# Attention with a residual on one core: the loads of x go to a step's last quarter, and one exchange round goes ahead of a result's stores

## The chip, the core and the metric

The kernel runs on one core of a Trainium2 chip. The core has a matrix engine (TensorE, "PE" in the profile; "PEld" are its weight loads), a vector engine (VectorE, DVE), a scalar engine (ScalarE, ACT), GpSimd (POOL) and SyncE (SP). SyncE computes nothing here; nearly every DMA is issued from its queue ("SPq"). All engines run side by side and wait for each other through semaphores. The metric is the device time of one execution in microseconds (us).

## The reference, cut to what matters

x has the shape (8, 512, 512): 8 batches of 512 positions by 512 features, float32. There are 16 heads of 32 features.

```python
Q = split_heads(x @ Wq.T + bq)
K = split_heads(x @ Wk.T + bk)
V = split_heads(x @ Wv.T + bv)
tQ = split_heads(tokens @ Wq.T + bq)      # one token per batch, from cond
tK = split_heads(tokens @ Wk.T + bk)
scores = einsum('bhqd,bhkd->bhqk', Q + tQ, K + tK) / sqrt(32)
attn = softmax(scores, axis=-1)
out = einsum('bhqk,bhkd->bhqd', attn, V)
return x + merge_heads(out)
```

## The kernel before

**Steps and quarters.** The work is cut into 32 steps, t = 0 to 31. Step t belongs to batch b = t // 4 and to a group of four heads, r = t % 4 (128 features, one head on each 32 partitions). A loop (L1000) runs steps 1 to 28; the first and the last steps are written out by hand. A step has four quarters, i = 0 to 3. Each quarter has one "item" on TensorE (part of the projections q, k or v of the next batch, or "V", the weighted sum of the values of step t - 1), and around it work for two other steps:

- `row_max` (L550) computes the scores of step t + 1 for 128 query rows, four heads side by side (matmuls L579), and VectorE reduces them to row maxima `nmax` (L546, L588). `denominators` (L620) then has ScalarE take the exponentials with that maximum and sum them (L634).
- `exponentials` (L681) computes the scores of step t a second time, transposed, with the row maxima subtracted by a small matmul (L686, which reads `maxT`), and ScalarE writes the exponentials `e` (L700). They are the moving operand of "V" in the next step (`times_v`, matmuls L709).
- `maxT` comes from GpSimd, which splits the maxima into bfloat16 parts (`split_max`, L642 to L651), and a transposing DMA on SyncE's queue (`turn_max`, L660).

**The blocked steps.** For t = 3, 7, ..., 27 (`BLOCKED`, L71; called u below, r = 3) the second computation of the scores is saved. The exponentials of `denominators` are kept in a big tile `blocks`. VectorE transposes it in 32 x 32 blocks (`turn_blocks`, L594, instruction L599, eight per step), and DMAs then exchange blocks between the partition groups (`swap_blocks`, L604, DMAs L618). The exchange is done in two halves. Each half has three rounds of six DMAs of 128 KB: round 0 copies blocks aside into `between`, round 1 copies the opposite blocks over them, round 2 copies `between` to the free places. A round's DMAs need those of the round before. Only when all six rounds have landed can "V" of step u begin, which is the last item of step u + 1 (there the items are q, k, v, V; in all other steps V, q, k, v). The table `SWAPS` (L991) says at the end of which quarter a round is recorded: the key is (t - u, i), the value (half, round).

```python
    SWAPS = {
        (-1, 2): (0, 0),
        (-1, 3): (0, 1),
        (0, 0): (0, 2),
        (0, 3): (1, 0),
        (1, 0): (1, 1),
        (1, 1): (1, 2),
    }
```

**x.** A block of x (128 features of a batch, 512 positions) is loaded by four DMAs of 64 KB into one of three buffers (`load_block`, L164, DMAs L170). VectorE transposes it into `xT` (`turn_x`, L345, instruction L351), and the call that has turned block n then loads block n + 3 into the buffer that has come free. In the loop, `turn_x` is called twice at the end of quarter 0 of the steps with r = 0 (that is step u + 1) and r = 1. GpSimd forms sums of parts of `xT` for the projections (`combine_x`, L354).

**Results.** After "V", VectorE transposes the result (`send`, L770, instruction L773), GpSimd multiplies by the reciprocal of the sums and adds the residual `xr` (L774, L775), and four DMAs store it (L778). The residual of step t + 1 (x with the bias of v) is loaded by four DMAs (`load_residual`, L179, DMAs L188) at the end of step t, and GpSimd adds the bias (L196).

**Who sets the order.** The order on TensorE, ScalarE, VectorE and GpSimd is the order in which the program is written (`manual_schedule`). SyncE's queue is not in that list: the framework places its DMAs, near where they are recorded. The queue is in order, and each DMA also waits for the one that stands eight places ahead of it to land.

Of the kernel before, what the change touches and what calls it, by code (L numbers as in the profile page):

```python
# [17 lines left out]
def kernel(  # L18
# [38 lines left out]
    nc = tc.nc  # L57
# [8 lines left out]
    NC = D // P  # L66
# [50 lines left out]
    def banks(i, n=1):  # L117

        row = row_of[0] or [at_end[j] for j in TURNS[turn[0]]]
        j = row[i]  # L120
        if n == 1:
            return psum[:, j, :]
        k = row[i + 1]
        return psum[:, j : k + 1 : k - j, :]
# [4 lines left out]
    def advance():  # L129
        turn[0] += 1  # L130
# [29 lines left out]
    def spread(a, d):  # L160

        return a.rearrange("(f j) d -> j f d", j=BL)[:, :, d : d + BL]

    def load_block(n):  # L164

        b, cc = divmod(n, NC)
        if b < B:
            xs[n] = xp.tile([P, NB, BL], F32, tag="x", name=f"x_{n}")
            for h in range(HG):
                nc.sync.dma_start(xs[n][h * BL : (h + 1) * BL], spread(x[b], cc * P + h * BL))  # L170
# [4 lines left out]
    def turned_by_vector(t):  # L175

        return t < T - 1

    def load_residual(t):  # L179

        b, g = divmod(t, G)
        if turned_by_vector(t):
            if late:
                xr[t] = late[0][:, 2, :].rearrange("p (f e) -> p f e", e=BL)
            else:
                xr[t] = op.tile([P, NB, BL], F32, tag="xr", name=f"xr_{t}")
            for h in range(HG):
                nc.sync.dma_start(  # L188
                    xr[t][h * BL : (h + 1) * BL], spread(x[b], g * P + h * BL)
                )  # L190
            bias = bvs[:, g, :].unsqueeze(1).broadcast_to([P, NB, BL])
        else:

            xr[t] = xT[b][:, g, :]
            bias = bvl.broadcast_to([P, S])
        nc.gpsimd.tensor_tensor(xr[t], xr[t], bias, ALU.add)  # L196
# [75 lines left out]
    for i in range(NS):  # L272
        r = slice(i * BL, (i + 1) * BL)
# [71 lines left out]
    def turn_x(n):  # L345
        b, cc = divmod(n, NC)
        if b >= B:
            return
        if cc == 0:
            xT[b] = xtp.tile([P, NC, S], F32, tag="xT", name=f"xT_{b}")  # L350
        nc.vector.transpose(xT[b][:, cc, :], xs[n].rearrange("p f i -> p (f i)"))  # L351
        load_block(n + 3)

    def combine_x(b, half, on=nc.vector):  # L354

        if b >= B:
            return
        blk = [[xT[b][:, i * 2 : i * 2 + 2, j * HS : (j + 1) * HS] for j in range(2)] for i in range(2)]
        to = [xc[:, i, :, :] for i in range(4)]
        if half == 0:  # L360
            on.tensor_tensor(to[2], blk[1][1], blk[0][1], ALU.subtract)
            on.tensor_tensor(to[1], to[2], blk[0][0], ALU.add)
        else:
            on.tensor_tensor(to[0], blk[0][1], blk[0][0], ALU.subtract)
            on.tensor_tensor(to[3], blk[1][0], to[1], ALU.subtract)
# [238 lines left out]
    def swap_blocks(t, half, move):  # L604

        def part(a, g):
            e = blocked[t][a * BL : (a + 1) * BL, g, half * 2 : half * 2 + 2]
            return e.rearrange("p c h s -> p (c h s)")

        if move == 0:  # L610
            between[t, half] = [
                ep.tile([P, 2, S], F32, tag="e", name=f"between_{t}_{half}_{i}") for i in range(2)
            ]
        for n, (a, g) in enumerate(APART):
            at = (n + 2) % HG * BL
            kept = between[t, half][n // HG][at : at + BL].rearrange("p i s -> p (i s)")
            to, of = [(kept, part(a, g)), (part(a, g), part(g, a)), (part(g, a), kept)][move]
            nc.sync.dma_start(to, of)  # L618
# [83 lines left out]
    def times_v(t, kc, pt, chunks=range(NS)):  # L702
        b, g = divmod(t, G)
        for j in range(HG):
            if t in BLOCKED:
                e = blocked[t][:, :, :, j, kc * BL : (kc + 1) * BL].rearrange("p a c e -> p c a e")
            else:
                e = es[t, kc, j // 2][:, j % 2, :]
            nc.tensor.matmul(  # L709
                pt[j * HD : (j + 1) * HD, :],  # L710
                vs[b % 2][:, kc, (g * HG + j) * HD : (g * HG + j + 1) * HD],
                e,
                start=(kc == chunks[0]),
                stop=(kc == chunks[-1]),
            )
# [13 lines left out]
    def masked(t):  # L729

        if t in aparts:
            return aparts.pop(t)
        apart = op.tile([P, HG, NS, NS], F32, tag="apart", name=f"apart_{t}")
        nc.gpsimd.tensor_tensor(
            apart,
            sums[t].rearrange("p c h o -> p h c o").broadcast_to([P, HG, NS, NS]),
            which.unsqueeze(1).unsqueeze(1).broadcast_to([P, HG, NS, NS]),
            ALU.mult,
        )
        return apart  # L740
# [16 lines left out]
    def weighted(t, pt, pd, between):  # L757

        apart = masked(t)
        for kc in range(NS):
            times_v(t, kc, pt)
            if kc == 0:
                spread_sums(apart, pd)
        rec = reciprocals(t, pd)
        between()
        send(t, pt, rec)
# [123 lines left out]
    split_max(0)  # L892
    first_products("k", 0, 1, lambda: denominators(0, 3), nothing, 2, 3)
    turn_x(NC)
    advance()
    row_max(1, 0)
    transpose_max(0, banks(1), nc.scalar.copy)
    other_products("k", 0, 1, lambda: denominators(1, 0), nothing, (0, 2))
    turn_x(NC + 1)
    load_residual(0)  # L900
    advance()

# [37 lines left out]
    row_max(1, 1)  # L940
    first_products("v", 0, 0, lambda: denominators(1, 1), nothing, 1)
    turn_x(NC + 2)
    load_residual(1)
    turn_x(NC + 3)
    advance()
    exponentials(0, 1)
    row_max(1, 2)
# [35 lines left out]
    def turn_more(t, i, late):  # L983

        for u in (t, t + 1):
            if u in BLOCKED:
                n = turned.get(u, 0)
                turned[u] = n + TURNED[t + 1 - u][i][late]
                turn_blocks(u, range(n, turned[u]))

    SWAPS = {  # L991
        (-1, 2): (0, 0),
        (-1, 3): (0, 1),
        (0, 0): (0, 2),
        (0, 3): (1, 0),
        (1, 0): (1, 1),
        (1, 1): (1, 2),
    }

    for t in range(1, T - 3):  # L1000
        b, r = divmod(t, G)
        blocks = t in BLOCKED
        w = 0 if blocks else HG
        items = ["q", "k", "v", "V"] if t - 1 in BLOCKED else ["V", "q", "k", "v"]
        for i, item in enumerate(items):
            rows = (t + 1, i + 1) if i < 3 else (t + 2, 0)
            begin(w)
            if not blocks:
                exponentials(t, i)
            late_first = item in ("v" if blocks else "qkv") and t % 2 == 1  # L1010
            hold = row_max(*rows, late_first, w)

            def held(i=i, hold=hold):
                hold()
                if i == 2:
                    split_max(t + 1)
                    turn_max(t + 1)

            dens = lambda: denominators(*rows, w)
            if item in "qkv":  # L1020
                products(t, item, blocks, held, dens, nothing)
            else:
                held()
                dens()
                if blocks:
                    weighted(t - 1, banks(4), banks(5), lambda: turn_more(t, i, 0))
                    released(6, 7, 0, 1, 2, 3, 5, 4)
                else:
                    weighted(t - 1, banks(0), banks(1), lambda: turn_more(t, i, 0))
                    released(2, 3, 1, 4, 5, 6, 7, 0)  # L1030
            if i == 0:
                if r == 0:
                    turn_x(t + NC + 2)
                    turn_x(t + NC + 3)
                if r == 1:
                    turn_x(t + NC + 3)
                    turn_x(t + NC + 4)
                if r == 1:
                    combine_x(b + 1, 1, nc.gpsimd)
            if i == 1 and r == 0:  # L1040
                combine_x(b + 1, 0, nc.gpsimd)
            if i == 2:
                aparts[t] = masked(t)
            if i == 3:
                load_residual(t + 1)
            turn_more(t, i, 1)
            for u in (t - 1, t, t + 1):
                if u in BLOCKED and (t - u, i) in SWAPS:
                    swap_blocks(u, *SWAPS[t - u, i])
    row_of[0] = None  # L1050

    def latest_pair(of, among):
# [64 lines left out]
    t = T - 3  # L1117
# [19 lines left out]
    t = T - 2  # L1137
# [26 lines left out]
    t = T - 1  # L1164
# [47 lines left out]
    b, g = divmod(t, G)  # L1212
# [55 lines left out]
```

## Time and profile before

| | us |
|---|---|
| median of 3 runs | 719.58 (717.72 to 719.66) |
| the profiled execution, its own time | 720.05 |
| its span in the trace | 718.0 |
| PE busy | 685.8 (96%) |
| VectorE busy | 563.6 (79%) |
| ScalarE busy | 563.2 (78%) |
| GpSimd busy | 233.2 (32%) |
| DMA queue of SyncE and ScalarE, share of the 16 DMA engines' time | 45.5% |

The profile is of one execution, whose time is 0.47 us above the median of the runs; 2.05 us of it lie outside the span. A busy time says how long an engine had an instruction in it, not that it was at its peak. "Idle before, releaser" is the time in which an engine stood still ahead of an instruction, and what the trace shows to have ended it; with a wait for several semaphores it is the one that came last by the profile. PEclk is the clock that TensorE was granted, 1.00 being full speed.

### The profile page before, as it was taken

What the parts mean: (1) busy time and instruction counts of PE and PEld (TensorE: products, weight loads), DVE (VectorE), ACT (ScalarE), POOL (GpSimd) and SP (SyncE); (2) the same over time, 40 slices, a digit from 0 to 9 for tenths busy, and PEclk for the clock granted to TensorE, in tenths of its full rate; (3) what the DMA queues carried; (4) which work ended last, traced back from release to release, by engine and by line L of the source; (5) the groups of instructions that cost most, each with busy time, mean ns of one, the idle gap of its engine ahead of it and who ended that gap; (6) DMA issues with size and microseconds to landing.
All of it is one profiled execution on the core that took longest, in us unless ns stands there. A gap on an engine that the chain in (4) does not pass through costs nothing.

```text
span 718.0 us, 22033 instructions
## 1 busy us (share of the span) xinstructions
PE 685.8 (96%) x8824; PEld 314.0 (44%) x8824; DVE 563.6 (79%) x878; ACT 563.2 (78%) x1427; POOL 233.2 (32%) x315
## 2 busy tenths in 40 slices
PE   9999999979999899989999899998999999999997
PEld 7444444424445344443444444443444445444432
DVE  3798798846988579884798857986689976987677
ACT  2589888858878688895888967888687998888664
POOL 3711323314243142421424233142431424231271
PEclk9999999999999999998999999999999999999999
DMA  6632426625267333673337723467225543177311
GB/s 178 106 54 47 68 36 151 140 61 82 42 146 150 67 65 75 127 156 55 58 70 133 163 48 57 99 125 148 47 46 116 121 101 63 34 152 148 53 31 30
DMA packets 231674, 65.50 MB, mean 91 GB/s; under 512 B 221834, under 2 KB 222346, under 8 KB 231572
## 3 DMA queue, kind: packets, MB, share of 16 engines
q1 hardware_dynamic: 229812, 63.05, 45.5%
q8 instruction: 69, 1.13, 0.7%
q10 hardware_dynamic: 1760, 1.05, 0.5%
q14 instruction: 33, 0.27, 0.1%
HBM read 19.75 MB, written 8.39 MB: 39 GB/s over the span
## 4 chain that ended last, share of the span: by engine, by line
PE 76%; SPq 7%; DMA 6%; POOL 4%; DVE 2%; ACT 2%; issue 2%; DVEq 0%; POOLq 0%; ACTq 0%
PE psum L435 30%; PE psum L709 16%; PE psum L579 13%; PE psum L689 9%; PE psum L686 4%; DMA maxT<-split 3%; SPq L618 2%; PE psum L378 2%; SPq L778 2%; SPq L170 2%; ACT psum L634 1%; DMA blocks<-between 1%; DVE nmax L546 1%; DMA xr<-in_x_dram 1%; POOL res L775 1%
## 5 line engine op out<-in xcount | busy, mean ns | idle before, releaser
L634 ACT ACTIVATE psum<-psum,nmax 128x512 f32<-128x512 f32 x368 | 244.5, 673 | 29.0 <-DVE nmax L546 21.5
L700 ACT ACTIVATE e<-psum 128x512 f32<-128x512 f32 x376 | 194.1, 603 | 91.2 <-PE psum L689 87.7
L546 DVE TENSOR_REDUCE nmax<-psum 128x1 f32<-128x512 f32 x298 | 191.3, 683 | 83.8 <-PE psum L579 81.4
L579 PE MATMUL psum<-kT,qT 32*128 32x512 f32 x1024 | 143.0, 605 | 0.0
L588 DVE TENSOR_REDUCE nmax<-psum 128x2 f32<-128x1024 f32 x101 | 122.5, 1213 | 1.3 <-PE psum L579 1.3
L689 PE MATMUL psum<-qT,kT 32*128 32x512 f32 x752 | 96.7, 587 | 0.0
L709 PE MATMUL psum<-e,v 128*32 128x512 f32 x800 | 95.3, 597 | 0.0
L196 POOL TENSOR_TENSOR xr<-xr,bvs 128x512 f32<-128x512 f32 x30 | 38.4, 1280 | 165.7 <-DMA xr<-in_x_dram 165.7
L774 POOL TENSOR_TENSOR res<-res,recs 128x512 f32<-128x512 f32 x30 | 31.4, 1047 | 179.3 <-DVE res L773 168.8
L579 PEld LDWEIGHTS psum<-kT,qT 32*128 32x128 f32 x1024 | 60.4, 182 | 53.1 <-issue 24.2
L634 ACT ACTIVATION_READ_ACCUMULATOR psum<-psum,nmax 128x1 f32 x368 | 78.8, 214 | 0.0
L634 ACT ACTIVATE blocks<-psum,nmax 128x512 f32<-128x512 f32 x112 | 76.1, 717 | 0.0
L599 DVE STREAM_TRANSPOSE blocks<-blocks 128x1024 f32<-128x1024 f32 x56 | 68.5, 1223 | 0.0
L709 PE MATMUL psum<-blocks,v 128*32 128x512 f32 x224 | 33.6, 741 | 17.9 <-ACT psum L634 10.9
L435 PE MATMUL psum<-wc_v,xc 128*32 128x256 f32 x768 | 50.2, 379 | 0.0
L435 PE MATMUL psum<-xc,wc_q 128*32 128x256 f32 x720 | 47.1, 379 | 0.0
L435 PE MATMUL psum<-xc,wc_k 128*32 128x256 f32 x720 | 47.1, 379 | 0.0
L686 PE MATMUL psum<-maxT,onesb 3*128 3x512 bf16 x376 | 37.1, 385 | 7.1 <-DMA maxT<-split 7.1
L709 PEld LDWEIGHTS psum<-e,v 128*32 128x32 f32 x800 | 20.8, 110 | 51.4 <-issue 29.2
L773 DVE STREAM_TRANSPOSE res<-psum 128x512 f32<-128x512 f32 x28 | 20.1, 717 | 29.1 <-PE psum L709 26.1
L775 POOL TENSOR_TENSOR res<-res,xr 128x512 f32<-128x512 f32 x30 | 38.5, 1283 | 2.4
L689 PEld LDWEIGHTS psum<-qT,kT 32*128 32x128 f32 x752 | 37.4, 185 | 1.7
(179 smaller groups left out, 877.4 us busy)
## 6 DMA issues: line engine op xcount, KB each, us to landing
between<-blocks SPq DMA_DIRECT2D x84, 128.0 KB, 2.4
blocks<-blocks SPq DMA_DIRECT2D x84, 128.0 KB, 2.3
blocks<-between SPq DMA_DIRECT2D x84, 128.0 KB, 2.4
out_dram<-res SPq DMA_DIRECT2D x122, 64.0 KB, 1.9
xr<-in_x_dram SPq DMA_DIRECT2D x120, 64.0 KB, 2.4
x<-in_x_dram SPq DMA_DIRECT2D x112, 64.0 KB, 2.4
w_q<-in_L_cond_Wq_dram SPq DMA_DIRECT2D x4, 256.0 KB, 4.8
w_v<-in_L_cond_Wv_dram SPq DMA_DIRECT2D x16, 64.0 KB, 2.3
```

The source lines that it names most:

```text
L196: nc.gpsimd.tensor_tensor(xr[t], xr[t], bias, ALU.add)
L435: nc.tensor.matmul(pt[r], still[:, r], moving, start=(kc == kcs[0]), stop=(kc == kcs[-1]))
L546: nc.vector.tensor_reduce(nmax[t][:, qc, j : j + 1, 0], pt, AX.X, ALU.max, negate=True)
L579: nc.tensor.matmul(pt, qkT["q", t][r, qc * P : (qc + 1) * P], qkT["k", t][r, :], start=True, stop=True,)
L588: nc.vector.tensor_reduce(nmax[t][:, qc, pr * 2 : pr * 2 + 2, 0], pt, AX.X, ALU.max, negate=True)
L599: nc.vector.transpose(e, e)
L634: nc.scalar.activation(to, of, AF.Exp, bias=nmax[t][:, qc, j, :], accum_out=sums[t][:, qc, j, :],)
L686: nc.tensor.matmul(bank[j], onesb[r, :], maxT[t][r, :], start=True, stop=False)
L689: nc.tensor.matmul(bank[j], qkT["k", t][r, kc * P : (kc + 1) * P], qkT["q", t][r, :], start=False, stop=True,)
L700: nc.scalar.activation(e[:, i, :], bank[pr * 2 + i], AF.Exp)
L709: nc.tensor.matmul(pt[j * HD : (j + 1) * HD, :], vs[b % 2][:, kc, (g * HG + j) * HD : (g * HG + j + 1) * HD], e, start=(kc == chunks[0]), ...
L775: nc.gpsimd.tensor_tensor(y, y, xr.pop(t), ALU.add)
```

## The change

`turn_x` no longer loads; it puts the number of the next block into a list, and `load_blocks` issues the loads of that list. In the loop `load_blocks` is called at the end of quarter 3 of every step. The two `turn_x` of the steps with r = 1 go from the end of quarter 0 to the end of quarter 2. Round 2 of the exchange's first half is recorded at the end of step u - 1, directly behind round 1, where it was recorded at the end of quarter 0 of step u. In a blocked step, the call of `turn_more` inside "V" is replaced by an empty one; by the table `TURNED` it turned no block there. Ahead of the loop each `turn_x` is directly followed by a `load_blocks`.

```diff
         nc.vector.transpose(xT[b][:, cc, :], xs[n].rearrange("p f i -> p (f i)"))
-        load_block(n + 3)
+        to_load.append(n + 3)
+
+    to_load = []
+
+    def load_blocks():
+        while to_load:
+            load_block(to_load.pop(0))
...
     SWAPS = {
-        (-1, 2): (0, 0),
-        (-1, 3): (0, 1),
-        (0, 0): (0, 2),
-        (0, 3): (1, 0),
-        (1, 0): (1, 1),
-        (1, 1): (1, 2),
+        (-1, 2): [(0, 0)],
+        (-1, 3): [(0, 1), (0, 2)],
+        (0, 3): [(1, 0)],
+        (1, 0): [(1, 1)],
+        (1, 1): [(1, 2)],
     }
...
                 if blocks:
-                    weighted(t - 1, banks(4), banks(5), lambda: turn_more(t, i, 0))
+                    weighted(t - 1, banks(4), banks(5), nothing)
...
-            if i == 0:
-                if r == 0:
-                    turn_x(t + NC + 2)
-                    turn_x(t + NC + 3)
-                if r == 1:
-                    turn_x(t + NC + 3)
-                    turn_x(t + NC + 4)
-                if r == 1:
-                    combine_x(b + 1, 1, nc.gpsimd)
+            if i == 0 and r == 0:
+                turn_x(t + NC + 2)
+                turn_x(t + NC + 3)
+            if i == 0 and r == 1:
+                combine_x(b + 1, 1, nc.gpsimd)
             if i == 1 and r == 0:
                 combine_x(b + 1, 0, nc.gpsimd)
+            if i == 2 and r == 1:
+                turn_x(t + NC + 3)
+                turn_x(t + NC + 4)
+            if i == 3:
+                load_blocks()
...
-                    swap_blocks(u, *SWAPS[t - u, i])
+                    for swap in SWAPS[t - u, i]:
+                        swap_blocks(u, *swap)
```

More of the change, by code (lines that the diff above doesn't have):

```diff
@@ L899 @@
     turn_x(NC + 1)
+    load_blocks()
     load_residual(0)
@@ L942 @@
     turn_x(NC + 2)
+    load_blocks()
     load_residual(1)
     turn_x(NC + 3)
+    load_blocks()
     advance()
@@ L1030 @@
                     released(2, 3, 1, 4, 5, 6, 7, 0)
-            if i == 0:
-                if r == 0:
-                    turn_x(t + NC + 2)
-                    turn_x(t + NC + 3)
-                if r == 1:
-                    turn_x(t + NC + 3)
-                    turn_x(t + NC + 4)
-                if r == 1:
-                    combine_x(b + 1, 1, nc.gpsimd)
+            if i == 0 and r == 0:
[3 more added lines that the diff above has]
+                combine_x(b + 1, 1, nc.gpsimd)
             if i == 1 and r == 0:
                 combine_x(b + 1, 0, nc.gpsimd)
+            if i == 2 and r == 1:
+                turn_x(t + NC + 3)
+                turn_x(t + NC + 4)
+            if i == 3:
+                load_blocks()
             if i == 2:
```

## The prediction

> **What bounds the kernel now.** First I asked what TensorE, busy 96% of the span, waits for. The waits of TensorE are three large groups and little else (us in total, times, longest):
>
> ```profile
> PE psum L709 <- ACT psum L634: 10.9, 3, 4.0
> PE psum L686 <- DMA maxT<-split: 7.1, 7, 1.8
> PE psum L709 <- DMA blocks<-between: 7.0, 2, 3.5
> ```
>
> The page's chain gives TensorE 76%, but a chain also runs through work that a short wait hangs on, so it does not size anything. I cut the loop instead into batches, each from the start of "V" of a blocked step to the next such start (TensorE's columns: stretch, its length, busy us and instructions, granted clock, DMA share, GB/s):
>
> ```profile
> 149.17:236.67 87.50, 83.17 (x1105) 0.98 0.49 96
> 236.67:324.55 87.88, 83.26 (x1105) 0.97 0.49 96
> 324.55:413.72 89.17, 84.28 (x1105) 0.97 0.49 95
> 413.72:500.55 86.83, 81.56 (x1105) 1.00 0.50 97
> 500.55:583.66 83.11, 83.11 (x1105) 0.98 0.45 91
> 583.66:666.30 82.64, 81.49 (x1109) 1.00 0.47 89
> ```
>
> The same instructions take 81.5 us of TensorE where the clock is full. The last two batches have almost no gap; the first four end with one. VectorE is busy 66 to 69 us and ScalarE 67 to 72 us of a batch, so a batch of 81.5 us is TensorE's own. The timeline shows where the gaps lie: ahead of "V" of u = 3, 7, 11, 15 and 19, never of u = 23 and 27. For u = 3 and u = 23, SyncE's queue and then TensorE (start, us, what; in brackets the idle before):
>
> ```profile
> 128.76 3.71 SPq L618 DMA_DIRECT2D between<-blocks  x6
> 132.57 1.17 SPq L618 DMA_DIRECT2D blocks<-blocks  x2
> 134.29 5.02 SPq L170 DMA_DIRECT2D x<-in_x_dram  x8
> 139.35 2.42 SPq L618 DMA_DIRECT2D blocks<-blocks  x4
> 141.81 4.74 SPq L618 DMA_DIRECT2D blocks<-between  x6
> 149.17 1.93 PE L709 MATMUL psum<-blocks,v 128*32 128x512 f32 x8 [3.92 <-ACT psum L634]
> ...
> 568.07 4.93 SPq L618 DMA_DIRECT2D between<-blocks  x6
> 573.10 3.74 SPq L618 DMA_DIRECT2D blocks<-blocks  x6
> 576.88 4.25 SPq L618 DMA_DIRECT2D blocks<-between  x6
> 583.66 1.07 PE L709 MATMUL psum<-blocks,v 128*32 128x512 f32 x8
> ```
>
> The last exchange DMA for u = 3 is issued by 146.55 us and a landing takes 2.2 to 4.4 us, so "V" starts when it lands; ScalarE, named in the bracket, is not the cause (for u = 23 "V" starts ahead of that step's L634). For u = 23 no block of x is left to load, and there is no gap. That is the change already made, once, in this trace.
>
> **Part 1, the eight loads of x leave the exchange.** In the built order of the changed kernel the second half's eighteen DMAs stand together; two loads, the transpose of `maxT` and six loads follow. The window from round 0's issue to TensorE's arrival (start of "V" less its idle) is 16.5, 15.7, 15.7, 16.0 and 15.7 us for u = 3 to 19. What the exchange needs without the loads is its issue time less the stretch the loads took (5.6, 5.2, 4.6, 5.7, 5.4 us), plus the landing (2.3 to 2.8): 14.6, 13.6, 15.4, 14.2 and 14.2 us. Measured directly it is about 15.4 us for u = 23 (window 15.6) and 14.7 for u = 27 (window 16.8). All fit, two of them only by 0.1 to 0.3 us. So the five waits go: 3.92 + 2.99 + 3.99 + 3.46 + 3.50 = 17.86 us. What is late next is the exchange itself at u = 11 or an arrival that is sooner; I keep 1 us back.
>
> **The clock.** Behind a gap "V" of u runs slower. From its start to the next L686 it takes 5.24, 5.33, 6.29, 3.63 and 5.32 us after the five gaps, and 3.63 at u = 23. The granted clock in that stretch is 0.69, 0.69, 0.57, 1.00 and 0.68. The excess is 1.61 + 1.70 + 2.66 + 0 + 1.69 = 7.66 us, and it goes with the gaps; bounds are 0 (gaps stay) and 7.66. The Trainium skill ("TensorE: Matmul & The Clock Gate", "HAM oscillation") has the clock halved after an idle of more than some 3.4 us; here 2.99 us was enough once and 3.46 once was not, and by the rule's own 3.4 us at half speed after each gap the term would be an estimated 8.5 us.
>
> **Part 2, the loads of r = 1.** Seven waits of L686 for `maxT` sum to 7.06 us. Four end steps with r = 1: 1.33, 0.63, 0.95 and 1.76. There the queue runs so:
>
> ```profile
> 168.31 2.56 SPq L778 DMA_DIRECT2D out_dram<-res  x4
> 170.93 2.96 SPq L170 DMA_DIRECT2D x<-in_x_dram  x5
> 173.94 0.49 SPq L188 DMA_DIRECT2D xr<-in_x_dram  x1
> 174.53 1.20 SPq L660 DMA_TRANSPOSE maxT<-split  x1
> 177.10 0.39 PE L686 MATMUL psum<-maxT,onesb 3*128 3x512 bf16 x4 [1.33 <-DMA maxT<-split]
> ```
>
> `split` was ready at 171.9. The new order is four stores, four loads of `xr` (2.1 us and a gap), `maxT`, then eight loads. From the stores' end to `maxT` the queue took 3.66, 4.33, 3.30 and 3.32 us; it will take 2.2. That is 1.46, 2.13, 1.10 and 1.12 sooner, enough for all but 0.64 us of the fourth: 4.03 us gained, bounds 0 and 4.67. The eight loads behind `maxT` (4.5 to 5.6 us) end by 179, and the queue then stands until the stores at 186.21.
>
> **Part 3, the first half's round 2 ahead of the stores.** Round 2's last five DMAs were issued at 119.39, behind stores that waited until 117.39 for their result; now they go at once, at 115.2, and the stores end near 120.3. `maxT` waits for `split` until 123.26, so the stores' delay costs nothing (3 us of cover; beyond it, each us delays `maxT`). What changes is the landing of that `maxT`, which took 4.17, 3.88 and 4.56 us behind exchange DMAs where TensorE waited (0.76, 0.48 and 1.15), against a shortest of 2.4. With an idle queue ahead of it I take all three, 2.39 us; bounds 0 and 2.39.
>
> **What is moved and costs nothing.** Two transposes of x (1.26 us together) leave VectorE's quarter 0 of r = 1 for the end of quarter 2. There VectorE idles 1.34 us for TensorE ahead of the maxima at 172.64; without that cover they would delay row maxima by 1.26 us in six steps, 7.6 us. Their data, formerly loaded during the exchange, is issued some 15 us ahead of the new place. At r = 0 `maxT` now has two loads (1.0 us) ahead of it, but `split` is only ready at 143.77, after they are issued, and 5.1 us ahead of its reader; its longest landing is 4.6. The six loads behind it end near 148.5; the stores they could delay are wanted at 157.77 less the 5.5 us gained, 152.2. Order and number of instructions on TensorE, ScalarE and GpSimd do not change. The Trainium skill ("DMA: Bandwidth & Descriptors", "Issuing engines are not separate DMA queues") calls the sequencer's issue time small beside the DMA; that speaks against Part 1, for then eight loads fewer in the queue would free next to nothing and the time would stay near 720. The rows say otherwise: an exchange DMA holds the queue 0.59 us of a 2.3 us landing, and eighteen of them are 11 to 13 us.
>
> **The sum.** 17.86 + 7.66 + 4.03 + 2.39 - 1 = 30.9 us off the profiled execution's 720.05: 689.0. As a control: the five batches up to 583.66 take 434.5 us, and five of 81.5 take 407.5, which is 27.0; with the gap at 149.17 (3.9) and two waits for `maxT` outside (0.76, 1.15) it is 32.8, all of which would give 687.2. The profiled execution is 0.5 us above the median of the runs and 2.3 above the lowest; the low end is the lowest run, 717.72, less all 32.6.
>
> **The rivals.** *The exchange still ends late.* Uninterrupted rounds may be as slow as the slowest sixes in the trace: 5.02, 4.82 and 4.74 us, with gaps and a landing 17.6 us against windows near 15.7. A wait of 1.9 us stays in five batches, 9.5 us less the 1 us already kept back: 697.6, or 704 if the waits for `maxT` stay too. For it: u = 23 fits by 0.1. Against: of the two uninterrupted trios in the trace the slower took 13.1.
>
> *Slower: the loads hold up SyncE's queue elsewhere.* The six loads at r = 0 now stand ahead of the stores of "V" of u, and behind those stores hang `xr`, GpSimd's additions, the next stores and the `maxT` of r = 1. Cover is 152.2 - 148.5 = 3.7 us. Every us beyond it is waited in five batches, so the gain of 31 is gone once the loads end 3.7 + 6.2 = 9.9 us late. If each load took the longest single issue, 1.91 us, eight would take 15.3 instead of 4.9, 10.4 late: 5 x 6.7 = 33.5 us, 722.5. Against: in the five groups of eight a load held the queue 0.56 to 0.70 us.
>
> *It does nothing:* the exchange is bound by landing and traffic, which stay the same (DMA share 0.69 from 128 to 150 us), and the time is 718 to 720. Against: from 566 to 590 us, without the loads, no wait is left.
>
> **How the numbers follow.** My forecast (686 to 693) has 0.78, the late exchange (693 to 706) 0.15, nothing 0.03, the held queue 0.04. The range 685 to 700 leaves out the two last and the worse part of the second. A change under 0.3% (2.2 us) cannot be told from none here. Faster 0.94, same 0.02, slower 0.04.
>
> **What would show it.** Right: seven batches near 81.5 us, no idle above 1 us ahead of L709 on `blocks`, a clock of 1.00 there, eighteen exchange DMAs issued in some 12 us, `maxT` of r = 1 issued 2.2 us after the stores' end. Wrong: idle left ahead of `blocks` though the loads are gone; new waits of L686 at r = 2; VectorE idle ahead of L351 in quarter 2 of r = 1; a longer wait of GpSimd for `xr`.

## The result and the profile after

The changed kernel takes 689.84 us (median of 4 runs, 689.37 to 692.37) against 718.66 for the kernel before (717.72 to 719.66; the three runs above and a fourth of 717.75): ratio 0.9606 [0.9577, 0.9635]. The forecast was 689.0. The profiled execution took 689.72 us, its span 687.9 in place of 718.0. Later runs, on chips 0, 11 and 14, show the kernel before at medians of 721.88 to 723.86, so each experiment below is read by its ratio to the runs of before made beside it. Line numbers from L353 to L894 are 6 higher in the changed kernel: "V" is L715, the exchange L624, `maxT` L666, its reader L692, the stores L784.

From the page of the changed kernel, the span, the busy times and the chain by engine:

```profile
span 687.9 us, 22054 instructions
PE 677.3 (98%) x8824; PEld 311.7 (45%) x8824; DVE 563.3 (82%) x878; ACT 563.7 (82%) x1427; POOL 233.3 (34%) x315
PE 88%; DMA 3%; POOL 3%; SPq 2%; ACT 1%; DVE 1%; issue 1%; DVEq 0%; POOLq 0%; ACTq 0%
```

The other engines' busy times are those of before to 0.5 us; TensorE's fell by 8.5 us with the same 8824 matmuls, so they ran faster. Its waits (us in total, times, longest):

```profile
PE psum L692 <- DMA maxT<-split: 2.3, 3, 1.1
PE psum L823 <- DVE onesb L239: 1.1, 1, 1.1
PE psum L692 <- ACT psum L640: 0.7, 1, 0.7
```

The two groups that waited for the exchange, 17.9 us, are gone. The waits for `maxT` are 3.05 us in four places, the 0.7 that names ScalarE being one. The batches, cut as before (stretch, its length, busy of TensorE, its weight loads, VectorE, ScalarE and GpSimd, granted clock, DMA share, GB/s):

```profile
144.40:226.92 82.52, 81.50 (x1109) 36.89 (x1105) 68.81 (x106) 70.84 (x183) 27.55 (x38) 1.00 0.52 102
226.92:308.34 81.42, 81.42 (x1109) 37.30 (x1105) 68.80 (x106) 70.84 (x183) 27.64 (x38) 1.00 0.53 104
308.34:391.13 82.79, 81.56 (x1109) 37.06 (x1105) 68.89 (x106) 70.84 (x183) 27.63 (x38) 1.00 0.52 102
391.13:472.58 81.45, 81.45 (x1108) 37.27 (x1104) 68.80 (x106) 70.83 (x183) 27.60 (x38) 1.00 0.53 104
472.58:554.11 81.53, 81.53 (x1108) 37.23 (x1104) 68.90 (x106) 70.84 (x183) 27.68 (x38) 1.00 0.50 99
554.11:636.47 82.36, 81.56 (x1108) 37.11 (x1105) 66.48 (x103) 71.01 (x183) 25.08 (x36) 1.00 0.46 90
```

Length and TensorE's busy time agree to 0.1 us in three batches; the other three hold one wait for `maxT` each. The timeline at u = 3, of SyncE's queue and then of TensorE:

```profile
128.49 3.70 SPq L624 DMA_DIRECT2D between<-blocks  x6
132.29 4.82 SPq L624 DMA_DIRECT2D blocks<-blocks  x6
137.15 3.76 SPq L624 DMA_DIRECT2D blocks<-between  x6
140.96 1.17 SPq L170 DMA_DIRECT2D x<-in_x_dram  x2
143.02 1.22 SPq L666 DMA_TRANSPOSE maxT<-split  x1
144.28 3.34 SPq L170 DMA_DIRECT2D x<-in_x_dram  x6
151.41 2.78 SPq L784 DMA_DIRECT2D out_dram<-res  x4
154.23 2.10 SPq L188 DMA_DIRECT2D xr<-in_x_dram  x4
162.08 3.11 SPq L784 DMA_DIRECT2D out_dram<-res  x4
165.23 2.10 SPq L188 DMA_DIRECT2D xr<-in_x_dram  x4
167.79 1.20 SPq L666 DMA_TRANSPOSE maxT<-split  x1
...
144.40 1.07 PE L715 MATMUL psum<-blocks,v 128*32 128x512 f32 x8
```

The eighteen exchange DMAs stand together and are issued in 12.4 us; "V" has no bracket, so no idle ahead of it. The six loads end at 147.62 and the stores come at 151.41: 3.8 us of cover. `maxT` of r = 1 follows the stores' end by 2.60 us here and by 2.28, 2.24, 2.26, 3.33 and 2.50 later.

### The profile page after: what moved, and what is told of

The parts are those of the page before. It is cut to its first block, busy times and chain, and to the rows that moved or that the text cites. A ratio compares the mean times of both kernels' runs of the same rounds, so it can differ in the third digit from the quotient of the medians.

```text
span 687.9 us, 22054 instructions
## 1 busy us (share of the span) xinstructions
PE 677.3 (98%) x8824; PEld 311.7 (45%) x8824; DVE 563.3 (82%) x878; ACT 563.7 (82%) x1427; POOL 233.3 (34%) x315
## 3 DMA queue, kind: packets, MB, share of 16 engines
q8 instruction: 69, 1.13, 0.7%
## 4 chain that ended last, share of the span: by engine, by line
PE 88%; DMA 3%; POOL 3%; SPq 2%; ACT 1%; DVE 1%; issue 1%; DVEq 0%; POOLq 0%; ACTq 0%
PE psum L441 37%; PE psum L715 16%; PE psum L585 16%; PE psum L695 11%; PE psum L692 4%; PE psum L384 2%; DMA maxT<-split 2%; SPq L784 1%; ACT psum L640 1%; SPq L188 1%; DMA xr<-in_x_dram 1%; POOL res L781 1%; DMA w_q<-in_L_cond_Wq_dram 1%; DVE nmax L552 1%; PE psum L725 1%
## 5 line engine op out<-in xcount | busy, mean ns | idle before, releaser
L715 PE MATMUL psum<-e,v 128*32 128x512 f32 x800 | 95.3, 597 | 0.0
L196 POOL TENSOR_TENSOR xr<-xr,bvs 128x512 f32<-128x512 f32 x30 | 38.4, 1280 | 141.8 <-DMA xr<-in_x_dram 141.8
L715 PEld LDWEIGHTS psum<-e,v 128*32 128x32 f32 x800 | 20.8, 110 | 51.4 <-issue 29.2
L692 PE MATMUL psum<-maxT,onesb 3*128 3x512 bf16 x376 | 37.1, 385 | 3.0 <-DMA maxT<-split 2.3
L441 PE MATMUL psum<-wT_v,xT 128*32 128x256 f32 x512 | 36.8, 382 | 0.0
```

Of the source, the lines that this page charges most:

```text
L441: nc.tensor.matmul(pt[r], still[:, r], moving, start=(kc == kcs[0]), stop=(kc == kcs[-1]))
L692: nc.tensor.matmul(bank[j], onesb[r, :], maxT[t][r, :], start=True, stop=False)
L715: nc.tensor.matmul(pt[j * HD : (j + 1) * HD, :], vs[b % 2][:, kc, (g * HG + j) * HD : (g * HG + j + 1) * HD], e, start=(kc == chunks[0]), ...
```

## The experiments

### One part at a time

The kernel before with the r = 0 loads alone moved:

```diff
-        load_block(n + 3)
+        to_load.append(n + 3)
+        if now:
+            load_blocks()
...
-                    turn_x(t + NC + 2)
-                    turn_x(t + NC + 3)
+                    turn_x(t + NC + 2, False)
+                    turn_x(t + NC + 3, False)
...
+            if i == 3:
+                load_blocks()
```

The calls of r = 1 keep `now=True` and load at once, as before.

> The kernel before, with one part of the change alone: the eight loads of x of the steps with r = 0 are issued at the end of quarter 3, behind the exchange. The loads and transposes of r = 1 and round 2 of the first half stay as before. My theory (the loads hold SyncE's queue in the middle of the exchange): the five gaps ahead of V of the blocked step go with the half clock behind them, 17.9 + 7.7 = 25.5 us, so about 693 us against 718.7, a ratio of 0.965; the waits for maxT (7.1 us in all) stay as they are. Rival (the exchange is bound by landing and traffic, and the gain of the whole change comes from its parts working together): gaps of 2 us or more stay, above 705 us.

Measured: ratio 0.9642 [0.9588, 0.9695], span 692.4, granted clock 0.999, no idle ahead of "V" of any blocked step. The waits of TensorE, whose largest is now

```profile
PE psum L694 <- DMA maxT<-split: 7.4, 7, 2.2
```

stay at the 7.1 of before. So the loads in the exchange, with the clock, are worth what the sum gave them (17.86 + 7.66 = 25.5 us would be 0.9646), and what is left to gain lies in the waits for `maxT`.

The second edit is to the kernel before and moves round 2 of the first half alone, with `SWAPS` as in the change:

> The kernel before with only round 2 of the first half moved ahead of the result's stores. The prediction's part 3: the maxT of r = 3 lands in 2.4 us where it took 3.9 to 4.6, TensorE's waits for it (0.76, 0.48, 1.15 us) go, 716.3 us, ratio 0.997. Rival, from the trace after the change: the landing of the same three (u = 3, 15, 27) is still 3.7, 4.5 and 4.1 us with an idle queue ahead of it; it is stretched by the transfers of TensorE's instructions (kind instruction on q8, one about every 9.4 us), which fall behind those three issues in both kernels; then the landing stays at 3.7 to 4.6 us and at most 0.4 us is gained, ratio 0.999 to 1.001.

Measured: ratio 1.0007 [0.9978, 1.0035]. `maxT` of r = 3 still lands late at u = 15 and 27, in 4.53 and 3.96 us, though the stores now stand between the exchange and it, and TensorE still waits 0.78 us at u = 3. Its waits at r = 3 sum to 2.50 us where they were 2.39. (All its waits for `maxT` sum to 10.0 us in this trace; how far that sum scatters is seen below.) Part 3 of the prediction falls.

The third edit, again to the kernel before, moves the two transposes of r = 1 to the end of quarter 2 and their loads to the end of quarter 3:

> The kernel before with only the r = 1 part: two transposes of x go from quarter 0 to the end of quarter 2 and their eight loads to the end of quarter 3. The prediction's part 2: maxT of r = 1 is issued 2.2 us behind the stores' end and lands 1.1 to 2.1 us sooner, 4.0 us gained, 714.6 us, ratio 0.9945; the five gaps ahead of V of the blocked step stay at 3 to 4 us. Rival: what is gained ahead of the gap is lost in it, because the exchange does not come sooner; then the gaps grow by about 0.8 us each and the ratio is 1.000.

Measured: ratio 0.9943 [0.9909, 0.9978], or 4.1 us, the size expected. The trace bears out only half of it: the waits for `maxT` go from 7.1 to 5.0 us, and at r = 1 from 4.67 to 3.5, of which 2.13 us stand at u = 7, where the four stores ahead of `maxT` took 3.50 us of queue in place of 1.99. The waits ahead of `blocks` stay (3.75, 2.66, 3.92, 4.05 and 3.11 us, 0.4 us less in all), but the clock is 1.00 behind the one of 2.66 us, and "V" to the next reader of `maxT` takes 1.2 us less over the five. The three ratios multiply to 0.959, beside 0.9606 for the whole change: within their intervals the parts add up.

The last of this kind is the changed kernel without its third part:

```diff
-        (-1, 3): [(0, 1), (0, 2)],
+        (-1, 3): [(0, 1)],
+        (0, 0): [(0, 2)],
```

> The changed kernel, with round 2 of the exchange's first half put back to the end of quarter 0 of step u, behind the result's stores. Theory now (the move of that round is worth nothing, since the late landing has another cause): ratio 0.961 as for the whole change, the waits of L692 near 3 us. By the prediction's third part it would lose 2.4 us: ratio 0.964, the waits near 5.4 us.

Measured: ratio 0.9566 [0.9537, 0.9596], waits for `maxT` of 4.1 us in all, 2.41 of them at r = 3. The changed kernel itself was run again later, on another chip and beside its own runs of before:

> The changed kernel itself, on the chip and beside the runs of the two others, as their measure: ratio 0.961 to the kernel before, waits of L692 near 3 us, slow landings of maxT at u = 3, 15 and 27.

Measured: 0.9571 [0.9529, 0.9613], waits of L692 of 5.0 us, 1.68 at r = 1 and 3.37 at r = 3. One landing of `maxT`, at u = 15, took 5.56 us this time and cost 2.16 of them. So two executions of the same kernel differ by 2.0 us in this sum, and a difference of that size between two traces shows little. With and without the third part the times cannot be told apart: it is worth nothing that these runs can see.

### Is it the queue, or the traffic?

The loads of r = 0 of the kernel before stay where they were, inside the exchange, but are issued by GpSimd. The bytes are those of before. They do not move in quite the same way: these forty loads go as 1280 packets of some 2 KB where SyncE's packets are of 128 bytes, and each lands 4.4 us behind its issue (median), against 2.4 for SyncE's loads of x before.

```diff
-                    turn_x(t + NC + 2)
-                    turn_x(t + NC + 3)
+                    turn_x(t + NC + 2, nc.gpsimd)
+                    turn_x(t + NC + 3, nc.gpsimd)
```

> The kernel before; the eight loads of x of the steps with r = 0 stay where they are in time, but are issued from GpSimd's queue. If the loads cost because they occupy SyncE's queue (my theory), the eighteen exchange DMAs are issued in some 12 us, and the gaps ahead of V of the blocked step go as in the run with the loads behind the exchange: about 693 us, or up to 5 us more if issuing holds GpSimd up so that maxT is late. If they cost because their traffic slows the exchange (rival), the gaps stay at 3 to 4 us and the time at 716 to 720 us.

Measured: ratio 0.9741 [0.9688, 0.9794]. At u = 11 the timeline of SyncE's queue, of GpSimd and of TensorE reads:

```profile
303.57 3.88 SPq L618 DMA_DIRECT2D blocks<-blocks  x6
307.49 4.49 SPq L618 DMA_DIRECT2D blocks<-between  x6
...
303.45 5.17 POOL L170 DMA_DIRECT2D x<-in_x_dram  x8 [2.98 <-DVE xT L351]
...
316.12 1.07 PE L709 MATMUL psum<-blocks,v 128*32 128x512 f32 x8 [1.98 <-ACT psum L634]
```

The exchange is issued with no break above 0.4 us here (its eighteen DMAs take 12.5 to 13.5 us at u = 3 to 19), while the loads run beside it. The five waits shrink from 17.9 to 0.82 + 1.02 + 1.98 + 1.12 + 1.20 = 6.1 us. So about two thirds of the gap go when the loads leave the queue. A third stays, and with it a slower landing: the last exchange DMA lands 3.8 to 4.9 us behind its issue at u = 3 to 15, against 2.3 to 2.5 with the loads behind the exchange. That points at the traffic, but since the loads' packets changed with their queue, the split is a rough one. The same loads behind the exchange cost neither.

### What slows the clock

In the kernel before, extra matmuls of a weight matrix with itself were written ahead of "V" of u = 3 to 19, into the bank that "V" overwrites. Six of them first:

```diff
         apart = masked(t)
+        if t in BLOCKED and t <= 19:
+            for _ in range(6):
+                nc.tensor.matmul(pt, wT["q"][:, 0, :P], wT["q"][:, 1, :], start=True, stop=True)
```

> The kernel before, with six extra matmuls written directly ahead of "V" of the five steps u = 3 to 19. They multiply constants into the bank that "V" then overwrites, so they leave the result alone and only keep TensorE at work for an estimated 2.6 us (six of 0.43 us) of the gap. The exchange and the loads are untouched, so "V" begins when it did. Theory (the slow clock behind the gap comes from TensorE's idling): the idle that is left is 0.4 to 1.4 us, the clock behind it is 1.00, "V" to the next L686 takes 3.6 us in place of 5.2 to 6.3, and up to 7.7 us go: ratio about 0.989. Rival ("V" is slow there because of what lands or for its own operands): the filler fills and nothing else changes, ratio 1.000.

Measured: ratio 0.9992 [0.9971, 1.0012]. The filler was mis-sized: each matmul stands in the trace as two instructions, together 0.9 us, so six fill 5.35 us and "V" came late. The clock behind them was 1.00, but the data had landed before the filler ended, so this says nothing against the rival. With three:

> The kernel before with three extra matmuls ahead of "V" of the steps u = 3 to 19, in place of six: each takes 0.89 us (two passes of 0.45), so three fill 2.7 us of a gap of 3 to 4. They leave the result alone. "V" begins when the exchange has landed, as in the kernel before. Theory (the slow clock comes from the idling): 0.3 to 1.3 us of idle is left, the clock behind it is 1.00, "V" to the next L686 takes 3.64 us, and 7.7 us go: ratio about 0.989. Rival ("V" is slow because of what has just landed or is still moving): 5.2 to 6.3 us as before, ratio 1.000.

Measured: ratio 0.9955 [0.9925, 0.9985]. "V" starts as its data lands, after an idle of 1.38, 0.48, 0.71, 1.41 and 0.55 us. The windows from the start of "V" to the next L686 (length, TensorE's busy us and instructions, clock, DMA share, GB/s):

```profile
149.44:153.08 3.64, 3.64 (x40) 1.00 0.00 0
236.17:239.81 3.64, 3.64 (x42) 1.00 0.02 5
323.35:326.98 3.63, 3.63 (x40) 1.00 0.03 6
410.30:413.93 3.63, 3.63 (x40) 1.00 0.01 1
499.94:503.58 3.64, 3.64 (x41) 1.00 0.00 0
```

In the kernel before the same stretches took 5.24, 5.33, 6.29, 3.63 and 5.32 us. The exchange and the loads are as before and "V" still starts on landing, 2.5 to 3.7 us behind the issue of the last exchange DMA (before: 2.6 to 3.2); only the idling is shorter. So the idling slows the clock, and the rival falls. The whole excess of 7.66 us is gone, but only 0.45% (3.2 us, by the interval 1.1 to 5.4) of the time, not 1.1%. The waits of this kernel say where most of the rest is:

```profile
PE psum L686 <- DMA maxT<-split: 11.5, 8, 2.4
```

They are 4.4 us longer than before, and filler and idle together are 18.7 us against 17.9: -7.66 + 4.4 + 0.9 = -2.4. Two of the eight are not due to the queue's order: behind u = 15 and u = 23, 2.45 and 1.09 us are waited for landings of 3.8 and 4.55 us, which took 2.5 and 2.6 in the kernel before and are stretched here by what the section after the next one describes. At u = 3, TensorE reaches the reader of r = 1's `maxT` 1.33 us sooner, and the queue issues that `maxT` only 0.88 us sooner (173.65 against 174.53), behind stores and loads that took 0.5 us longer. This holds for the old order of that queue; in the whole change the order at r = 1 moves too.

### The rival on the other side: how much room the queue has

In the changed kernel, the loads of r = 0 are issued three times:

```diff
-                load_blocks()
+                load_blocks(2 if r == 0 else 0)     # the same eight loads twice more
```

> The changed kernel, with the eight loads of x of the steps with r = 0 issued three times over (the same data to the same place, sixteen loads more in the queue of a batch). By the built order some four stand ahead of the first stores, twelve between these stores and the loads of xr, and two ahead of the next stores. Theory (the rival "held queue" of the prediction has the right cover): xr arrives 6 to 7 us later than in the changed kernel, GpSimd's additions, the next stores and the maxT of r = 1 follow, and behind a slack of 1 to 3 us TensorE waits 4 to 6 us at L692 in five or six batches: 20 to 35 us more, ratio 0.99 to 1.01, with no gap ahead of "V" of u. Other theory (the queue has far more room than the 3.7 us of cover): ratio below 0.97.

Measured: ratio 1.0123 [1.0083, 1.0163]. SyncE's queue behind u = 3 (L364 are the added loads, L188 `xr`, L672 `maxT`), and the largest wait of TensorE:

```profile
152.12 3.01 SPq L790 DMA_DIRECT2D out_dram<-res  x4
155.17 6.81 SPq L364 DMA_DIRECT2D x<-in_x_dram  x12
162.03 2.67 SPq L188 DMA_DIRECT2D xr<-in_x_dram  x4
166.29 0.85 SPq L170 DMA_DIRECT2D x<-in_x_dram  x2
170.02 1.97 SPq L790 DMA_DIRECT2D out_dram<-res  x4
173.64 1.20 SPq L672 DMA_TRANSPOSE maxT<-split  x1
```

```profile
PE psum L698 <- DMA maxT<-split: 30.5, 8, 6.0
```

`xr` is issued 7.8 us later than in the changed kernel, `maxT` of r = 1 is 5.85 us later, and TensorE waits 6.03 us at u = 3 where it waited 1.02. There is no idle ahead of "V" of u. The waits are 27.5 us longer, and TensorE's busy time is 10.7 us longer (688.0 against 677.3), since its clock is low behind such waits (0.66 in the 5.4 us behind the one at u = 3). The path of the rival is as the prediction drew it and costs more than the whole gain; that it did not come about is due to the number of loads, not to a queue that nobody waits for.

### Why `maxT` of r = 3 lands late

In the kernel before and in the changed one it is late at u = 3, 15 and 27 and at no other u, which is every third batch. At u = 15 the changed kernel's timeline of SyncE's queue and of TensorE reads:

```profile
365.01 2.20 SPq L784 DMA_DIRECT2D out_dram<-res  x4
368.93 1.22 SPq L666 DMA_TRANSPOSE maxT<-split  x1
...
373.45 0.40 PE L692 MATMUL psum<-maxT,onesb 3*128 3x512 bf16 x4 [1.08 <-DMA maxT<-split]
```

The queue is idle from 367.21 to 368.93, and the landing still takes 4.47 us. The page of the profile has a DMA queue whose size says that it moves TensorE's own program:

```profile
q8 instruction: 69, 1.13, 0.7%
```

1.13 MB is 64 bytes for each of 2 x 8824 matmuls and weight loads; 69 transfers are 16 KB, or by that 256 instructions, each. A batch has 2210 of them, 8.63 transfers, and three batches almost 26: the place of the transfers comes back every third batch. An experiment moves it by half a period:

```diff
-    for _ in range(28):
+    for _ in range(92):
         nc.tensor.matmul(warm[:, :P], onesb, onesb, start=True, stop=True)
```

> The changed kernel, with 64 more of the matmuls that warm TensorE up ahead of the work (each with its weight load, 128 instructions; they write nothing that is read). The start grows by an estimated 3.5 us. Everything later keeps its order. Theory (the maxT of r = 3 lands late where a transfer of TensorE's program, 16 KB once in about 9.4 us, falls into it): the transfers come half a period (4.7 us) earlier against the work, and the late landing leaves u = 3, 15 and 27 (2.4 us there) and may show at other steps. Rival (the late landing belongs to these steps): 3.6 to 4.5 us at u = 3, 15 and 27 as in the changed kernel. Ratio 0.962 to 0.967 by either.

Measured: ratio 0.9619 [0.9587, 0.9651]. From the trace's DMA records, the start of the nearest such transfer against the issue of `maxT` (us), and the landing behind that issue:

| `maxT` | changed kernel | shifted |
|---|---|---|
| r = 3, u = 15 | +1.9: 4.47 | -2.5: 3.56 |
| r = 3, u = 23 | -2.2: 2.44 | +1.9: 4.20 |
| r = 3, u = 27 | +1.3: 4.09 | -2.5: 2.47 |
| r = 1, u = 7 | -0.3: 2.89 | +2.0: 4.00 |
| r = 1, u = 15 | -3.6: 2.47 | +1.9: 4.17 |

u = 27 is cured and u = 23 is hit, at u = 3 TensorE no longer waits, and the waits at r = 1 rise: L692 waits 5.3 us in all. u = 15 stays late, with 3.56 us, and no transfer near it explains that. Over the thirteen traces of this study 220 landings of `maxT` are recorded. In 32 a transfer begins 1.0 to 2.0 us behind the issue (times here to 0.1 us): all 32 take 3.6 to 5.6 us, median 4.1. In 157 none begins from 0.5 us ahead to 2.6 us behind: median 2.48, and three take more than 3.3 us. That a landing is stretched when such a transfer falls into it is shown; by what means, the trace does not say.

A last version was to use this:

```diff
-    for _ in range(28):
+    for _ in range(14):
         nc.tensor.matmul(warm[:, :P], onesb, onesb, start=True, stop=True)
```

> The changed kernel with 14 in place of 28 of the matmuls that warm TensorE up. They run while it waits for the first weights, so the start does not get shorter; the transfers of TensorE's program come 28 instructions, about 1.0 us, later against the work. Theory: the maxT of u = 3, 15 and 27, now hit by a transfer 1.2, 1.9 and 1.3 us behind its issue, is hit after it has gone: all r = 3 landings near 2.5 us, the waits of L692 fall from 3.05 to 1 or 1.5 us, and the time by some 1.5 to 2 us against the changed kernel: ratio 0.997 to it. Rival: landings and waits as in the changed kernel.

Measured: ratio 0.9579 [0.9542, 0.9616], beside 0.9571 for the changed kernel against the same runs of before. The offsets at u = 15 and 27 are +2.0 and +1.3, the landings 4.25 and 3.83, the waits of L692 5.1 us. The place of the transfers scatters by about 1 us from kernel to kernel (TensorE's instructions begun ahead of the same transfer differ by up to 52, both ways, between this kernel and the changed one, and by up to 32 between two executions of the changed kernel), and a shift of 28 instructions drowns in that. No version here beats the changed kernel by anything measurable.

## Why the prediction was right, and where it was not

The time was right (689.0 against 689.84) and so was its main mechanism. By its steps:

- **Part 1, the loads in the exchange: 17.86 us.** Right. The gaps are 0 in the changed kernel and with the loads alone. The arrivals that were to fit "by 0.1 to 0.3 us" did fit; the 1 us kept back was not needed. In the second execution of the changed kernel the exchange took 13.8 us once, and "V" waited 0.13 us, so the fit is as narrow as it was drawn. About two thirds of the gap went with the loads' place in the queue alone; the prediction did not separate queue and traffic.
- **The clock: 7.66 us.** Right in size, and its cause is shown by the filler. The prediction weighed the Trainium skill's rule of some 3.4 us of idle ("TensorE: Matmul & The Clock Gate", "HAM oscillation"). These runs agree with the mechanism and not with a single length: an idle of 1.98 us was followed by a clock of 0.68 (the loads on GpSimd's queue, u = 11), one of 2.16 us by 1.00 (the changed kernel run again, u = 15).
- **Part 2, `maxT` of r = 1: 4.03 us.** Right in place, and near in size: 4.67 us of waits fell to 1.02, so 3.65 (to 1.68 in the second execution, so 3.0). One of the four waits, the 0.95 us behind u = 11, stood behind a landing of 3.93 us, which the prediction did not see. `maxT` came 2.2 to 2.6 us behind the stores in five of six batches, as worked out; in the sixth it was 3.33.
- **Part 3, `maxT` of r = 3: 2.39 us.** The term that was mis-sized, and its reason was wrong. The three late landings were laid to the exchange DMAs ahead of them and all counted as gained. With 1.0 to 1.7 us of idle queue ahead of them they still take 3.65 (by TensorE's start), 4.47 and 4.09 us. The waits went from 2.39 to 2.03 us (0.25, 1.08 and 0.70): 0.36 in place of 2.39, and they were 3.37 in the second execution. Moving the round by itself gave 1.0007, and taking it out of the change lost nothing. What the landings share is a transfer of TensorE's program. That they stood at u = 3, 15 and 27, and not at the other four steps with the same queue order, was in the trace of before and spoke against the reason given.
- **What is moved and costs nothing.** Right: no idle of VectorE stands ahead of its transposes of x in the changed kernel, and GpSimd waits 141.8 us for `xr` where it waited 165.7.
- **The sum.** The span fell by 30.1 us: 17.86 of gaps, 7.66 of clock, 4.0 of waits for `maxT` make 29.5. Part 3 came out 2.0 us short and Part 2 0.4; the 1 us kept back, and 0.8 us by which TensorE's busy time fell more than the clock term (8.5 against 7.66), made up for most of it. That these met is luck; the terms that carry the forecast, 25.5 of 31 us, are not. (The terms sum to 30.94, which gives 689.1, not the 689.0 written.)
- **The rivals.** The late exchange did not come about: trios of rounds were issued in 12.0 to 12.7 us up to u = 19, not in the 14.6 of its three slow sixes. The held queue has a cover of 3.8 us (3.7 worked out), and with sixteen loads more it turns the gain into 1.2% of loss. "It does nothing" had the Trainium skill on its side, which calls the issue time usually small beside the DMA ("DMA: Bandwidth & Descriptors", "Issuing engines are not separate DMA queues"). Here it was not small: the loads on another queue took 2.6% off with the same bytes.

## What to carry to other kernels

Where a chain of dependent DMAs sets a start, look at what else stands in the same in-order queue between its links: each foreign DMA adds its issue time to the chain. Here eight of them cost 3.6 us of waiting in a batch, some two thirds of it by their hold on the queue, and another 1.5 us of slow clock behind it. Before such DMAs are moved, follow who hangs behind the new place and how much cover there is, since a late residual load cost more here than the whole change brought. When a wait shows up at some repeats of the same code and not at others, do not explain it by what all repeats have in common.

## What was not expected of the hardware

TensorE's program is itself loaded by DMA during the run, 16 KB about every 9.4 us, and a `maxT` landing that such a transfer falls into takes 4.1 us in place of 2.5 (32 of 32 cases). Since a batch is 8.63 transfers long, three batches are almost a whole number of them, and the cost appears in every third batch. It is not removed by an idle queue, and a small shift of the program's length did not steer it.
